# A selective scan's first steps reordered: single delta steps in a spare tile, sums ahead of layer 0's last pieces, late weights loaded one by one

## The chip, the core and the metric

The kernel runs on one core of a Trainium2 chip. A core has five engines that run side by side, each with its own queue of instructions taken in order: TensorE (PE, matmuls into PSUM), VectorE (DVE), ScalarE (ACT), GpSimd (POOL) and SyncE (SP, which here only issues DMA transfers). The metric is device time in microseconds (us) of one execution, from three executions before the change: 904.06, 905.18 and 905.91 us, median 905.18.

## The reference

Two transformer-like layers over four sequences (b) of 256 tokens with 512 features. Layer 0 adds to x a latent attention of 32 heads and a gated feed-forward part. Layer 1 adds a selective state-space block and a mixture of low-rank experts. Only the state-space block, and the end of layer 0 before it, matter here:

```
proj = hidden @ in_proj_w;  x, z = split(proj)          # 1024 channels each
xc = silu(conv4(x))                                     # causal, 4 taps a channel
dt_r, Bm, Cm = rmsnorm of the parts of xc @ x_proj      # 32, 16, 16
dt = softplus(dt_r @ dt_proj + dt_bias)                 # the "delta steps"
h[t] = exp(dt[t] * A) * h[t-1] + dt[t] * Bm[t] * xc[t]  # per channel and 16 states
y[t] = sum over states of h[t] * Cm[t]
out = ((y + D * xc) * silu(z)) @ out_proj
```

softplus(v) is made as relu(v) + log(1 + exp(-|v|)), with a correction for the rounding of 1 + exp(-|v|).

## The kernel before

**Layer 0's end.** The feed-forward down projection of the second half of the tokens (`down(1, i)`, blocks 4 to 7 of 128 tokens) is a generator of 64 pieces: for each block one piece with the attention part (L437), fourteen pieces of two 128x512 matmuls (L442), and one that adds the result to x (L447) or, for the last blocks, leaves it in PSUM for `add_last` (L454). `go(ff, n)` puts the next n pieces into TensorE's queue. They are used as filling between layer 1's first work, by hand: 9 before the convolution, then 1 between its parts, 8, 3, 9, then 12 in each of steps 0 and 1, and the rest in step 2.

**The scan.** The 1024 channels of a sequence are 8 chunks (c) of 128; a chunk takes 4 steps, each for 4 of the 16 states, so that a sequence has 32 steps and the kernel 128. A step u works on tiles whose 128 partitions are 32 channels x 4 states, with four such blocks of 256 tokens side by side, and its parts lie on four engines:

- ACT: `decays` makes exp(dt * A) (L867), two steps ahead of the scan;
- DVE: `scan_in` makes bx (L873), then `scan` makes h with one scan instruction (L888);
- POOL: hc = h * C (L892);
- TensorE: `states_sum` adds hc over the states into ysum (L904), one step later; the D part (L902) opens a chunk.

After a chunk's last step `close_chunk` (L908) multiplies ysum by silu(z) (sz, made by `gate_silu`, which loads ACT's silu table and then the exponential one again). The channels of a chunk must be spread over partitions in another layout: dt and du = dt * xc are sent to DRAM (`send`, L821) and read back in pieces (`spread`, four issues each, L827) as dts and dus. Chunk 0 of the first sequence goes through TensorE instead (pdts, pdus: L1080, L1087), and chunk 1 is sent alone (L1092).

**Delta steps.** `step_in` makes a matmul pdt for two chunks and |v| and relu(v) on ACT (L784, L785); `step_exp` makes the exponential, 1 + it, and the logarithm on ACT (L793 to L796), in the tiles u, lw and e; `step_out` makes three sums on POOL, and `step_x` du on POOL. For chunks 2 and 3 of the first sequence this is done with chunk pairs: the first two before step 0 (L1100, L1101), the sums on POOL in steps 0 to 2.

**Borrowed tiles.** Layer 0's tiles lie where layer 1's large pool (`act`) will be. Until layer 0's last matmul is done, the first four steps borrow other tiles (L847): their decays, h and hc lie in the weight tiles w_in, and in u, lw and e. `open_act` (L1103) then closes layer 0's pool, makes decay tiles 1 and 2, and loads the weights for the end of the layer: rl, bw, lb and ow, 0.27, 1, 0.25 and 2 MB, one behind the other on SP (L1112).

**What else the first sequence's steps hold.** The loads of the z weights (`load_z`, 0.5 MB into w_in) and the matmuls pz from them (L836); the second sequence's layer norm (`norm_stats`, `norm_scale` with sh on DVE, L668, and xnt on ACT, `norm_turn`, `norm_copy`), its input projection px (L696) and convolution (ACT L704 to L712, DVE L720, POOL L726).

**The order.** Nothing is scheduled automatically: each engine's queue is the order in which the program calls. `put(b, s, f)` hangs a call into step s of sequence b ahead of the step's scan, `put_late` behind it, and one loop over the steps walks these lists:

```
for u in range(total + 2):
    if u < 2: go(ff, 12)
    if 3 <= u < total - 2: decays(u + 2)
    ... put calls, scan_in, close_chunk, scan ...
    if u == 2: open_act()
    if u < 3: decays(u + 2)
    ... put_late calls ...
    if 1 <= u <= total: states_sum(u - 1)
```

Of the kernel before, what the change touches and what calls it, by code (L numbers as in the profile page):

```python
# [8 lines left out]
F32 = mybir.dt.float32  # L9
# [8 lines left out]
P = 128  # L18
# [23 lines left out]
def block_kernel(  # L42
# [389 lines left out]
    def down(th, i):  # L432

        tb = 4 * th + i
        po = psmm.tile([P, D], F32, tag="mm", name="po")
        for hf in range(2):
            mm(po, lhsT=o8ns[th][:, hf, i * P : (i + 1) * P], rhs=m_att[:, hf, :],  # L437
               start=(hf == 0), stop=False)
        yield
        for m in range(MC):  # L440
            for j in range(2):
                mm(po, lhsT=hids[th][j][:, m, i * P : (i + 1) * P], rhs=wd[:, m, :],  # L442
                   start=False, stop=(m == MC - 1 and j == 1))
            if m < MC - 1 or th:
                yield
        if tb < 6:
            nc.vector.tensor_tensor(x[:, tb, :], x[:, tb, :], po, ALU.add)  # L447
        else:
            live["last", tb] = po
        yield  # L450
# [5 lines left out]
    def go(gen, n=1000):  # L456
        for _ in range(n):
            if next(gen, 1) == 1:
                break
# [327 lines left out]
    def step_exp(b, h, q=slice(0, 4)):  # L787
# [7 lines left out]
        nc.scalar.activation(e, w, AF.Identity, bias=eps[:, 2:3])  # L795
        nc.scalar.activation(w, w, AF.Ln)  # L796

    def step_out(b, h, q, k):
        s = slice(2 * q, 2 * q + 2)
        e, dt = live["e"][:, s, :], dts[b, h][:, s, :]  # L800
        if k == 0:
            nc.gpsimd.tensor_tensor(e, live["u"][:, s, :], e, ALU.subtract)
        elif k == 1:
            nc.gpsimd.tensor_tensor(e, e, live["lw"][:, s, :], ALU.add)
        else:
            nc.gpsimd.tensor_tensor(dt, dt, e, ALU.add)
            send("dt", b, 2 * h + q, dt)
# [11 lines left out]
    def send(n, b, p, t):  # L819
        live[n, b, p] = scr.tile([2, P, S], F32, tag=n, name=f"{n}d")  # L820
        nc.sync.dma_start(live[n, b, p].rearrange("c p t -> p c t"), t)  # L821
# [17 lines left out]
    def gate_silu(b, *ps):  # L839
# [5 lines left out]


    lent = {  # L847
        "d": ("d", "w_in", "d", "w_in"), "h": ("w_in", "u", "w_in", "u"),
        "hc": ("w_in", "lw", "e", "lw"),
    }  # L850

    def lend(n, u):
# [218 lines left out]
    for j, eng in ((0, nc.vector), (1, nc.gpsimd)):  # L1071
# [1 line left out]
        eng.tensor_tensor(e[:, j, :], e[:, j, :], lw[:, j, :], ALU.add)  # L1073
        eng.tensor_tensor(dt[:, j, :], dt[:, j, :], e[:, j, :], ALU.add)
        eng.tensor_tensor(du[:, j, :], dt[:, j, :], xcs[0][:, j, :], ALU.mult)
    go(ff, 9)

    pdts = psx.tile([P, NG, S], F32, tag="bx", name="pdts")
    for k in range(NG):
# [17 lines left out]
    b_rows(0, 1)  # L1097
    c_rows(0, 1)
    decays(1)
    step_in(0, 0, 1)  # L1100
    step_exp(0, 0, slice(2, 4))  # L1101

    def open_act():  # L1103
        nonlocal act
        l0.close()
        act = ctx.enter_context(tc.tile_pool(name="act", bufs=1))
        decay_tile(act)
        decay_tile(act)
        for n, shape, d in (("rl", [P, HC, NE + P], rl_d), ("bw", [P, HC, D], base_d),
                            ("lb", [P, D], lb_d), ("ow", [P, DC, D], ow_d)):  # L1110
            late_w[n] = act.tile(shape, F32, name=n)
            nc.sync.dma_start(late_w[n], d)  # L1112


    at, late_at = {}, {}
# [1 line left out]
    def put(b, s, f, *a):  # L1117
        at.setdefault(b * PER + s, []).append((f, a))

    def put_late(b, s, f, *a):  # L1120

        late_at.setdefault(b * PER + s, []).append((f, a))

    for b in range(B):
        nxt = b + 1
        if b:
            put(b, 0, b_rows, b, 1)
            put(b, 0, spread, "du", b, 1)

            for c in range(DC):  # L1130
                put(b, c // 2, out_mm, b - 1, 1, c)
            put(b, 3, out_x, b - 1, 1)
            put(b, 4, dense, b - 1, 0, 0)
            put(b, 5, dense, b - 1, 0, 1)
            put(b, 5, expert_out, b - 1, 0)
            for c in range(DC):
                put(b, 6 + c, out_mm, b - 1, 0, c)
            put(b, 15, out_x, b - 1, 0)
        else:
            for k in range(3):  # L1140
                put(b, k, step_out, b, 0, 1, k)
            put(b, 2, step_x, b, 1)
            put(b, 1, load_z, b, 0)
            put(b, 4, load_z, b, 1)
            for p, u in ((0, 2), (1, 6)):
                for i in range(2):
                    put(b, u, pz_mm, b, p, i)
            put(b, 2, go, ff)
            put(b, 4, gate_silu, b, 0)
            put(b, 8, gate_silu, b, 1)  # L1150
            put_late(b, 2, add_last, 6)
            put_late(b, 3, add_last, 7)
        if b:
            put(b, 0, gate_silu, b, 0, 1)

        o = 0 if b else 3
        put(b, 1 if b else 5, step_in, b, 1, 0)
        put(b, 2 if b else 6, step_in, b, 1, 1)
        put(b, 3 if b else 7, step_exp, b, 1)
        for q in range(2):  # L1160
            for k in range(3):
                put(b, 5 + o + 3 * q + k, step_out, b, 1, q, k)
        for p in (2, 3):
            put(b, 3 * p + 2 + o, step_x, b, p)
        for c in range(2, DC):
            o = 0 if b or c < 4 else 1
            put(b, 4 * c - 6 + o, spread, "dt", b, c)
            put(b, 4 * c - 4 + o, spread, "du", b, c)
        put(b, 10, load_z, b, 2)
        put(b, 12, load_z, b, 3)  # L1170
        for p, at_i, at_g in ((2, (14, 15), 16), (3, (19, 21), 23)):
            for i in range(2):
                put(b, at_i[i], pz_mm, b, p, i)
            if p == 3 or nxt == B:
                put(b, at_g, gate_silu, b, p)
        if nxt < B:
            o = 0 if b else 1
            put(b, 0 if b else 2, norm_stats, nxt)
            put(b, 2 + o, norm_scale, nxt)
            put(b, 3 + o, norm_turn, nxt, 0)  # L1180
            put(b, 4 + o, norm_copy, nxt, 0)
            put(b, 4 + o, norm_turn, nxt, 1)
            put(b, 5 + o, norm_copy, nxt, 1)
            for p in range(NP):
                put(b, 2 * p if b else (5, 6, 7, 8)[p], load_x, nxt, p)
                for i in range(2):
                    put(b, 6 + o + 2 * p + i, px_mm, nxt, p, i)
                put(b, 8 + o + 2 * p, conv_in, nxt, p)
                put(b, 9 + o + 2 * p, conv_taps, nxt, p)
            put(b, 16 + o, conv_silu, nxt, (b, 2))  # L1190
            put(b, 17 + o, pp_mm, nxt, 0)
            put(b, 18, pp_mm, nxt, 1)
            put(b, 19, pp_square, nxt)
            put_late(b, 20, pp_norm, nxt)
            put(b, 21, step_in, nxt, 0, 0)
            put(b, 22, step_in, nxt, 0, 1)
            put(b, 22, c_rows, nxt, 0)
            put(b, 23, step_exp, nxt, 0)
            put(b, 23, c_rows, nxt, 1)
            for q in range(2):  # L1200
                for k in range(3):
                    put(b, 24 + 3 * q + k, step_out, nxt, 0, q, k)
            put(b, 27, step_x, nxt, 0)
            put(b, 27, spread, "dt", nxt, 0)
            put(b, 29, spread, "du", nxt, 0)
            put(b, 30, step_x, nxt, 1)
            put(b, 30, b_rows, nxt, 0)
            put(b, 31, spread, "dt", nxt, 1)
            put(b, 23, load_z, nxt, 0)
            put(b, 25, load_z, nxt, 1)  # L1210
            for k, u in enumerate((27, 28, 29, 31)):
                put(b, u, pz_mm, nxt, k // 2, k % 2)
            if b % 2 == 0:
                for i, u in enumerate((16, 17, 18, 20)):
                    put(b, u, router, b, i)
                put(b, 22, route_exp, b)
                put(b, 23, route, b)
            put(b, 24, expert_turn, b)
            put(b, 25, dense, b, 1, 0)
            put(b, 26, dense, b, 1, 1)  # L1220
            put(b, 27, expert_out, b, 1)
        else:

            put(b, 12, expert_turn, b)
            put(b, 17, dense, b, 0, 0)
            put(b, 18, dense, b, 0, 1)
            put(b, 18, expert_out, b, 0)
            put(b, 20, dense, b, 1, 0)
            put(b, 21, dense, b, 1, 1)
            put(b, 21, expert_out, b, 1)  # L1230
# [1 line left out]
    total = B * PER  # L1232
    late = []
    for u in range(total + 2):
        if u < 2:
            go(ff, 12)
        if 3 <= u < total - 2:
            decays(u + 2)
        for f, a in at.get(u, ()):
# [9 lines left out]
                late.append(c)  # L1249
        if u < total:  # L1250
            scan(u, 1 if u < total - 1 else 4)
            if u == 2:
                open_act()
            if u < 3:
                decays(u + 2)
        for f, a in late_at.get(u, ()):
            f(*a)
# [3 lines left out]
                out_mm(B - 1, i, c)  # L1261
        if 1 <= u <= total:
            states_sum(u - 1)
    for i in range(2):
        for c in late:
            out_mm(B - 1, i, c)
        out_x(B - 1, i)
# [101 lines left out]
```

## Time and profile before

| what | value |
|---|---|
| median of three runs | 905.18 us |
| the profiled execution's own time | 904.87 us |
| its span, from first to last instruction | 903.1 us |
| PE, DVE, ACT, POOL busy | 749.8, 687.3, 525.4, 489.1 us |
| TensorE clock granted, mean | 0.93 |
| scan of step 0, 1, 2, 3, 4 starts (DVE L888) | 362.85, 369.70, 378.22, 384.23, 388.37 us |
| scan of step 5, 8, 9, 10, 16 starts | 393.44, 404.46, 414.91, 426.24, 452.23 us |
| layer 0's last matmul ends | 384.8 us |
| one bx, scan, hc, decay (four ACT instructions) | 1.24, 2.29, 2.35, 1.7 us |

All times of single instructions are in us from the start of the span of one profiled execution. In a timeline a line gives the start, the duration, the engine, the source line, the operation, what it writes and reads, and in brackets how long the engine had been idle before it and what ended that. In the chain of waits, a line is one stretch of the work that ended last, in order of time: start, duration, engine and line.

### The profile page before, as it was taken

Reading aid. Unit: us, or ns where it says so; the run is one execution under the profiler, and the core shown is the slowest. Engines: PE = TensorE matmul, PEld = TensorE weight load, DVE = VectorE, ACT = ScalarE, POOL = GpSimd, SP = SyncE. Lnnn points to the kernel's source line nnn. Section 1 sums busy time; section 2 is a strip of 40 time slices with the busy share of each in tenths; the row PEclk is TensorE's granted clock in tenths of the full one; section 3 lists DMA queues with packets and bytes.
Section 4 is the critical chain, followed back from the end, with each engine's and each line's share of the span. In section 5 each row is a group of like instructions: output and inputs, shape, how many; then the busy total and the mean of one; then the engine's idle time right before and its main releaser. Section 6 shows DMA issues by size and latency. Waiting matters only on the chain.

```text
span 903.1 us, 10448 instructions
## 1 busy us (share of the span) xinstructions
PE 749.8 (83%) x3554; PEld 432.4 (48%) x3554; DVE 687.3 (76%) x675; ACT 525.4 (58%) x1005; POOL 489.1 (54%) x374
## 2 busy tenths in 40 slices
PE   5999979999989999956785798787897877875875
PEld 3665545666556576733452434443444443322421
DVE  5685553476563423694998999999999999999996
ACT  4234455313437346468778497778687785765661
POOL 4222222001223341554965969868789749797664
PEclk9899999999999999969796999987999888989997
DMA  6232332001122241493523443632645323436300
GB/s 210 60 92 72 81 105 70 12 1 36 48 69 70 59 109 31 116 275 110 142 58 93 127 142 103 165 94 62 171 120 170 85 79 84 117 94 169 87 26 23
DMA packets 67343, 86.67 MB, mean 96 GB/s; under 512 B 12077, under 2 KB 52025, under 8 KB 66906
## 3 DMA queue, kind: packets, MB, share of 16 engines
q1 hardware_dynamic: 57930, 67.12, 26.6%
q0 software_dynamic: 9072, 18.35, 7.4%
q8 instruction: 28, 0.46, 0.2%
q10 hardware_dynamic: 288, 0.52, 0.2%
q14 instruction: 25, 0.20, 0.1%
HBM read 66.58 MB, written 10.22 MB: 85 GB/s over the span
## 4 chain that ended last, share of the span: by engine, by line
PE 38%; DVE 33%; ACT 15%; issue 4%; POOL 4%; DMA 4%; SPq 1%; DVEq 0%; ACTq 0%; POOLq 0%
DVE h L888 20%; ACT decay L867 7%; DVE bx L873 6%; PE po L442 5%; PE pu L417 5%; PE pg L417 4%; PE sc L329 4%; PE av L371 3%; PE scT L361 3%; PE pz L836 2%; POOL hc L892 2%; PE pp L740 2%; DMA w_in<-in_inz 1%; ACT pe L363 1%; PE ysum L904 1%
## 5 line engine op out<-in xcount | busy, mean ns | idle before, releaser
L892 POOL TENSOR_TENSOR hc<-h,cr 128x1024 f32<-128x1024 f32 (+1 forms) x131 | 301.8, 2306 | 111.0 <-DVE h L888 96.3
L888 DVE TENSOR_TENSOR_SCAN h<-decay,bx 128x1024 f32<-128x1024 f32 (+1 forms) x129 | 287.9, 2234 | 15.1 <-PE ysum L904 3.5
L867 ACT ACTIVATE decay<-dts,aneg 128x255 f32<-128x255 f32 x504 | 213.9, 498 | 130.3 <-DVE h L888 115.6
L904 PE MATMUL ysum<-hc,stack 128*32 128x256 f32 x1024 | 89.8, 420 | 94.9 <-POOL hc L892 94.5
L873 DVE TENSOR_TENSOR bx<-brow,dus 128x1024 f32<-128x1024 f32 x128 | 157.6, 1231 | 3.7
L429 POOL TENSOR_TENSOR hlo<-g,hhi 128x512 fp32r<-128x512 f32 x28 | 36.1, 1289 | 149.3 <-ACT hhi L428 149.3
L331 DVE TENSOR_REDUCE mpl<-sc 128x4 f32<-128x1024 f32 x64 | 77.2, 1222 | 23.9 <-PE sc L329 23.8
L904 PEld LDWEIGHTS ysum<-hc,stack 128*32 128x32 f32 x1024 | 21.6, 111 | 154.0 <-POOL hc L892 137.2
L400 POOL DMA_DIRECT2D wgu<-in_wgu x56 | 31.0, 553 | 92.4 <-PE pg L417 82.3
L363 ACT ACTIVATE pe<-scT 128x1024 f32<-128x1024 f32 x64 | 62.8, 1023 | 29.8 <-PE scT L361 29.5
L996 PE MATMUL po<-ow,xc 128*128 128x512 f32 x128 | 72.3, 674 | 2.7 <-DVE xc L908 2.7
L836 PE MATMUL pz<-xn1T,w_in 128*128 128x256 f32 x256 | 69.7, 421 | 4.4 <-DMA w_in<-in_inz 4.4
L696 PE MATMUL px<-xn1T,w_in 128*128 128x256 f32 x256 | 63.4, 394 | 2.2 <-ACT xn1T L688 1.6
L836 PEld LDWEIGHTS pz<-xn1T,w_in 128*128 128x128 f32 x256 | 50.5, 207 | 24.2 <-issue 11.1
L696 PEld LDWEIGHTS px<-xn1T,w_in 128*128 128x128 f32 x256 | 49.9, 198 | 21.6 <-issue 11.0
L425 DVE SCALAR_TENSOR_TENSOR g<-g,pg 128x512 f32<-128x512 f32 x28 | 19.2, 685 | 52.0 <-ACT g L424 52.0
L428 ACT CAST hhi<-g 128x512 fp32r<-128x512 f32 x28 | 17.4, 620 | 62.1 <-DVE g L427 61.8
L417 PE MATMUL pg<-xhi,wgu 128*128 128x512 f32 x112 | 46.8, 418 | 5.4 <-issue 2.9
L417 PE MATMUL pu<-xhi,wgu 128*128 128x512 f32 x112 | 47.8, 426 | 3.3 <-issue 1.5
L442 PE MATMUL po<-wd,hhi 128*128 128x512 f32 x112 | 48.8, 435 | 0.0
L329 PE MATMUL sc<-km,qg 128*128 128x512 f32 x128 | 43.9, 424 | 3.3 <-ACT pe L363 2.8
L417 PE MATMUL pg<-xlo,wgu 128*128 128x512 f32 x112 | 44.9, 401 | 0.0
(214 smaller groups left out, 1251.9 us busy)
## 6 DMA issues: line engine op xcount, KB each, us to landing
dts<-dtd SPq DMA_DIRECT2D x124, 128.0 KB, 2.9
dus<-dud SPq DMA_DIRECT2D x124, 128.0 KB, 3.0
wgu<-in_wgu POOLq DMA_DIRECT2D x56, 256.0 KB, 2.8
w_in<-in_inz SPq DMA_DIRECT2D x16, 512.0 KB, 4.8
w_in<-in_inx SPq DMA_DIRECT2D x15, 512.0 KB, 4.6
dtd<-dt SPq DMA_DIRECT2D x15, 256.0 KB, 2.2
dud<-du SPq DMA_DIRECT2D x15, 256.0 KB, 2.2
wd<-in_wd POOLq DMA_DIRECT2D x7, 512.0 KB, 3.6
```

Source lines behind the costliest of these rows:

```text
L329: mm(sc[:, hp, :], lhsT=qs[b][:, gq, hf, qb * P : (qb + 1) * P], rhs=kms[b][:, 2 * hp : 2 * hp + 2, :], start=True, stop=True)
L331: nc.vector.tensor_reduce(mpl2[b % 2][:, qb, :, 16 + 2 * gq + hf].rearrange("p (a i) -> p a i", a=2), sc.rearrange("p a (i k) -> p a i k", ...
L417: mm(ps, lhsT=wgus[i][:, hc, :], rhs=xs[j][:, hc, :], start=(hc == 0 and j == 0), stop=(hc == HC - 1 and j == 1))
L442: mm(po, lhsT=hids[th][j][:, m, i * P : (i + 1) * P], rhs=wd[:, m, :], start=False, stop=(m == MC - 1 and j == 1))
L696: mm(px[:, i, :], lhsT=w[:, i, hc, :], rhs=xns[b][:, hc, :], start=(hc == 0), stop=(hc == HC - 1))
L836: mm(pz[:, i, :], lhsT=w[:, i, hc, :], rhs=xns[b][:, hc, :], start=(hc == 0), stop=(hc == HC - 1))
L867: nc.scalar.activation(da[:, k, 1:], live["dts", b, c][:, k, 1:], AF.Exp, scale=aneg[:, c, k, g : g + 1])
L873: nc.vector.tensor_tensor(bx, brow[g // 2][:, g % 2, :].unsqueeze(1).to_broadcast([P, NG, S]), live["dus", b, c], ALU.mult)
L888: nc.vector.tensor_tensor_scan(h[:, n].rearrange("p n t -> p (n t)"), da[:, n].rearrange("p n t -> p (n t)"), bx[:, n].rearrange("p n t -> ...
L892: nc.gpsimd.tensor_tensor(hc[:, n], h[:, n], crows[b][:, g, :].unsqueeze(1).to_broadcast([P, NG // parts, S]), ALU.mult,)
L904: mm(ysum[k * NB : (k + 1) * NB, :], lhsT=stack, rhs=hc[:, k, :], start=False, stop=(g == NU - 1))
L996: mm(live["po", b, i], lhsT=xcs[b][:, c, i * P : (i + 1) * P], rhs=late_w["ow"][:, c, :], start=False, stop=(c == DC - 1))
```

## The change

- Ahead of pdts there are 5 pieces of layer 0 and not 9. In step 0, 9 pieces are put in, in step 1, 12, in step 2 the rest, each behind the step's scan and behind `states_sum` of the step before, not ahead of it. Block 5's sum joins those of `add_last`.
- The delta steps of chunks 2 and 3 are made one chunk at a time by `one_step` and `one_out`, in a tile `one` that has the convolution's tag "tap" (one buffer) in place of u, lw and e.
- In the first four steps h of step 2 lies in e and hc of step 2 in w_in (the other way round before).
- `open_act` makes the tiles of the late weights but doesn't load them; `load_late` loads rl, bw, lb and ow in steps 9, 11, 13 and 15. `open_act` and the decays of step 4 come at the end of step 2, behind the last pieces.
- `load_z` 0 comes behind step 2's scan, followed by the sends; the spread of chunk 2's dt in step 3; pz 0 in step 3; the norm statistics of the second sequence behind step 3's scan, its `norm_scale` and the first `norm_turn` one step or so later, the `norm_copy` calls behind the scan of step 5.

```diff
-        if tb < 6:
+        if tb < 5:
             nc.vector.tensor_tensor(x[:, tb, :], x[:, tb, :], po, ALU.add)
         else:
             live["last", tb] = po
...
+    def one_step(c):
+        pd = psmm.tile([P, 2, S], F32, tag="mm", name="pdt")[:, 0, :]
+        mm(pd, lhsT=dtw[:, c * P : (c + 1) * P], rhs=nrms[0][0:RK, :], start=True, stop=True)
+        t = live["one"] = w1.tile([P, KC - 1, S], F32, tag="tap", name="one")
+        u, w, e = (t[:, k, :] for k in range(3))
+        db = vec[:, c, V_DB : V_DB + 1]
+        nc.scalar.activation(u, pd, AF.Abs, bias=db)
+        nc.scalar.activation(dts[0, 0][:, c, :], pd, AF.Relu, bias=db)
+        nc.scalar.activation(u, u, AF.Exp, scale=-1.0)
+        nc.scalar.activation(w, u, AF.Identity, bias=1.0)
+        nc.scalar.activation(e, w, AF.Identity, bias=eps[:, 2:3])
+        nc.scalar.activation(w, w, AF.Ln)
+
+    def one_out(c):
+        u, w, e = (live["one"][:, k, :] for k in range(3))
+        dt = dts[0, 0][:, c, :]
+        nc.gpsimd.tensor_tensor(e, u, e, ALU.subtract)
+        nc.gpsimd.tensor_tensor(e, e, w, ALU.add)
+        nc.gpsimd.tensor_tensor(dt, dt, e, ALU.add)
...
     lent = {
-        "d": ("d", "w_in", "d", "w_in"), "h": ("w_in", "u", "w_in", "u"),
-        "hc": ("w_in", "lw", "e", "lw"),
+        "d": ("d", "w_in", "d", "w_in"), "h": ("w_in", "u", "e", "u"),
+        "hc": ("w_in", "lw", "w_in", "lw"),
     }
...
-    go(ff, 9)
+    go(ff, 5)
...
-    step_in(0, 0, 1)
-    step_exp(0, 0, slice(2, 4))
+    one_step(2)
...
-            late_w[n] = act.tile(shape, F32, name=n)
-            nc.sync.dma_start(late_w[n], d)
+            late_w[n] = act.tile(shape, F32, name=n), d
+
+    def load_late(n):
+        t, d = late_w[n]
+        nc.sync.dma_start(t, d)
+        late_w[n] = t
...
-            for k in range(3):
-                put(b, k, step_out, b, 0, 1, k)
-            put(b, 2, step_x, b, 1)
-            put(b, 1, load_z, b, 0)
+            put(b, 1, one_out, 2)
+            put(b, 1, one_step, 3)
+            put(b, 2, one_out, 3)
+            put_late(b, 2, load_z, b, 0)
+            put_late(b, 2, lambda: send("dt", 0, 1, dts[0, 0][:, 2:4, :]))
+            put_late(b, 2, step_x, b, 1)
             put(b, 4, load_z, b, 1)
-            for p, u in ((0, 2), (1, 6)):
+            for k, n in enumerate(("rl", "bw", "lb", "ow")):
+                put(b, 9 + 2 * k, load_late, n)
+            for p, u in ((0, 3), (1, 6)):
                 for i in range(2):
                     put(b, u, pz_mm, b, p, i)
-            put(b, 2, go, ff)
             put(b, 4, gate_silu, b, 0)
             put(b, 8, gate_silu, b, 1)
-            put_late(b, 2, add_last, 6)
-            put_late(b, 3, add_last, 7)
+            put_late(b, 1, add_last, 5)
+            put_late(b, 3, add_last, 6)
+            put_late(b, 4, add_last, 7)
...
-            put(b, 4 * c - 6 + o, spread, "dt", b, c)
+            put(b, 3 if c == 2 and not b else 4 * c - 6 + o, spread, "dt", b, c)
...
-            put(b, 0 if b else 2, norm_stats, nxt)
-            put(b, 2 + o, norm_scale, nxt)
-            put(b, 3 + o, norm_turn, nxt, 0)
-            put(b, 4 + o, norm_copy, nxt, 0)
-            put(b, 4 + o, norm_turn, nxt, 1)
-            put(b, 5 + o, norm_copy, nxt, 1)
+            if b:
+                put(b, 0, norm_stats, nxt)
+            else:
+                put_late(b, 3, norm_stats, nxt)
+            put(b, 2 if b else 4, norm_scale, nxt)
+            put(b, 3 if b else 5, norm_turn, nxt, 0)
+            (put if b else put_late)(b, 4 if b else 5, norm_copy, nxt, 0)
+            put(b, 4 if b else 5, norm_turn, nxt, 1)
+            (put if b else put_late)(b, 5, norm_copy, nxt, 1)
...
     for u in range(total + 2):
-        if u < 2:
-            go(ff, 12)
...
             scan(u, 1 if u < total - 1 else 4)
-            if u == 2:
-                open_act()
-            if u < 3:
+            if u < 2:
                 decays(u + 2)
         for f, a in late_at.get(u, ()):
             f(*a)
...
         if 1 <= u <= total:
             states_sum(u - 1)
+        if u < 3:
+            go(ff, (9, 12, 100)[u])
+        if u == 2:
+            open_act()
+            decays(4)
```

## The prediction

> **What bounds the kernel now.** I read the page, then the chain of waits and each engine's timeline from 350 to 500 us, the only stretch the edits touch. Of the page:
>
> ```profile
> span 903.1 us, 10448 instructions
> PE 749.8 (83%) x3554; PEld 432.4 (48%) x3554; DVE 687.3 (76%) x675; ACT 525.4 (58%) x1005; POOL 489.1 (54%) x374
> ```
>
> From about 424 us DVE is hardly idle (449.75 of the 479 us to the end busy; bx 1.24 and scan 2.29, 3.66 us a step), so a scan that starts earlier there ends the kernel earlier. Before that it isn't the bound: step 0's scan starts at 362.85 and step 10's at 426.24, 63.4 us where ten steps need 36.6. DVE's timeline shows the holes:
>
> ```profile
> 369.70 2.29 DVE L888 TENSOR_TENSOR_SCAN h<-d,bx 128x1024 f32<-128x1024 f32 x1 [3.30 <-POOL e L802]
> ...
> 378.22 2.29 DVE L888 TENSOR_TENSOR_SCAN h<-decay,bx 128x1024 f32<-128x1024 f32 x1 [3.51 <-PE ysum L904]
> ...
> 414.57 0.42 DVE L908 TENSOR_TENSOR xc<-ysum,sz 128x256 f32<-128x256 f32 x1 [6.55 <-PE ysum L904]
> ...
> 423.46 1.01 DVE L720 SCALAR_TENSOR_TENSOR px<-pad,vec,px 128x256 f32<-128x256 f32 x2 [6.28 <-ACT xc L707]
> ```
>
> The chain of waits names what is under the last two: a weight load issued behind the late weights (L1112), then TensorE, then ACT.
>
> ```profile
> 387.17 13.18 DMA w_in<-in_inz
> 400.34 0.14 issue
> 400.48 5.78 PE pz L836 x16
> 406.25 1.07 PE pdt L779 x4
> 407.32 0.02 issue
> 407.35 0.03 ACT u L784
> ```
>
> ACT's timeline shows its two long waits there:
>
> ```profile
> 384.86 3.30 ACT L867 ACTIVATE decay<-dts,aneg 128x255 f32<-128x255 f32 x8 [10.71 <-PE po L442]
> ...
> 407.35 0.47 ACT L784 ACTIVATE u<-pdt,vec 128x256 f32<-128x256 f32 x1 [7.75 <-PE pdt L779]
> ```
>
> And the issues of this stretch, with us to landing (the load above took 13.2):
>
> ```profile
> w_in<-in_inz SPq DMA_DIRECT2D x6, 512.0 KB, 4.8
> ...
> ow<-in_ow SPq DMA_DIRECT2D x1, 2048.0 KB, 11.4
> ```
>
> **What the Trainium skill says.** "TensorE: Matmul & The Clock Gate", What's actually happening: after an idle window of about 3.4 us TensorE runs at half clock, and at full again after such a time of sustained work. The trace agrees: the windows from 393 to 401 show a clock of 0.50, from 405 on 1.00, and L836 took 5.78 us at 400.48 but 3.72 at 377.92. The same page, Architectural detail, calls ACT's and DVE's queues strict FIFO: here DVE stood 6.55 us at L908 with its scan behind it. "DMA: Bandwidth & Descriptors", Queues, rings and completion order: each DMA engine takes a queue's descriptors in ring order; the 13.18 us beside a usual 4.8 agree.
>
> **The change, part by part** (times on the clock of the profile).
>
> *Five pieces instead of nine before pdts.* The 16 L442 matmuls at 353.37 end at 357.15; ten end at 355.75 (0.23 each), after DVE's dt (355.06). pdts, its copy, bx and scan 0 come 1.4 us earlier: scan 0 at 361.45. Block 5's sum (0.67) leaves an idle place on DVE for one behind scan 1. The sends of chunk 1 don't move (POOL's chain, 358.2).
>
> *Single steps in a spare tile.* ACT: twice 2.49 us (351.12 to 353.61 for chunk 0's six) for 4.06 (364.81 to 368.87); POOL: six of 0.81 for three of 1.28, plus 1.0. But POOL's hc 0 now stands directly behind scan 0 (363.8 to 366.2; before, 369.63), and the u tile is free, so the POOL wait of the first DVE line goes: scan 1 at 361.45 + 3.65 = 365.1. A new wait: the spare tile has one buffer, so ACT's second step waits for POOL's third add on the first (366.2 + 3 x 0.8 = 368.6); queued behind it on ACT is decay 3 (368.6 + 2.5 + 1.65 = 372.75), for which DVE asks at 372.8.
>
> *Sums in front of the pieces, h of step 2 in the e tile.* hc 0 is summed at 368.5 (before 377.35), and scan 2 no longer needs its buffer: with the moved sum of 0.67, scan 2 at 369.25 (378.22), scan 3 at 372.9 (384.23), 11 us ahead.
>
> *Where that gain goes.* Decays 1 and 2 lie in the pool that opens when layer 0's last matmul is done (the 10.71 above). TensorE is busy without a gap from 353.37 to 384.83, 31.5 us; pz 0 (3.65) now follows the pieces and ysum 1 (0.57) precedes the last of them, so 28.4, and it ends near 381.9: 2.9 earlier only. What its new order makes it wait for is early: hc 0 (366.2) for ysum 0, hc 1 (368.6 + 2.4) for ysum 1 at 375, block 5's sum (368.0) for the place of block 7's po at 373. ACT's decays 4 and 5 (3.3) and then rsn (0.52) end at 385.75. DVE's sh (L668) now stands ahead of bx 4 and waits for rsn; Four statistics moved behind scan 3 (1.7) fall into that hole. sh itself took 0.13 twice and 1.98 once under a POOL hc; POOL is idle then, so 0.13. bx 4, scan 4 at 387.3, against 388.37: 1.1 left of 11. Block 7's sum, sz and close 0 put scan 5 at 391.6 (393.44).
>
> *z 1 without the late weights.* The four L1112 issues (1.7 us) leave SP's queue there, and dts of chunk 2 goes out behind dud with z 1 behind it; z 0 is issued after step 2, not in step 1. On SP: z 0 after ysum 0 (368.6), dtd (373.5), dud behind POOL's hc 2 and du (377.2), chunk 2's dts, z 1 at 379.5, dus; z 1 lands near 384 (4.8), dts and dus of chunk 2 by 385, and decay 8 asks at 396. x 0 (behind pz 0, 385.7, landing 390.5) and x 1 (behind decay 7 and ysum 2, 395.8, landing 400.6) are early for the px matmuls of 403 to 409. So pz 1 waits for something else: the PSUM place that ACT frees. ACT from 385.75: decay 6 (1.65), table, sz, table (3.2), two xnt (1.5), decay 7 (1.65), four steps of pdt (1.45): 395.2. pz 1 starts 5.3 us earlier than 400.48. TensorE idles some 3.6 us from 387.8, as it did before, so I take its 5.78 and pdt's 1.07 again; bounds 3.65 (full clock) and 7.3 with 2.1 (half throughout). ACT's second four steps: 402.1 (407.35).
>
> *From there ACT sets the pace, as before*: 407.35 to the taps at 423.46 is 16.1 us, less one xn1T copy (0.46), now ahead of decay 8: taps at 417.75, 5.7 us earlier. close 1 waits for ysum 7, which TensorE reaches behind pdt, two ysum and two half px (402.1 + 5.6 = 407.7), so it is done by 408.1, scan 9 by 410.5, and both hide in front of the taps.
>
> *rl, bw, lb, ow in steps 9 to 15.* Four issues of 0.4 us on SP, where it waits anyway. On the old clock ow goes out at 446.8 right before dts of chunk 5, for which ACT asks at 461.4: 14 us. Both together: at the rate of the old burst (3600 KB from 385.2 to 398.0) 2560 KB take 9 us; above, 11.4 + 2.9 = 14.3; below, an estimate by the page's 2.0 us plus bytes over 436 GB/s (Anatomy of one DMA, given for the other DMA path): 8. So nothing; that cover gone, each us late is a us on ACT and the scans. dus of chunk 5 waits for ow's landing too and has till 465.7. rl (step 16) and bw (step 25) are early.
>
> Sum: nothing before 353, -5.7 at step 10, kept over the DVE-bound rest. The profiled execution took 904.87 (span 903.1 and 1.8 around it): 899.2. The median is 0.3 above it: 905.18 - 5.7 = **899.5 us**.
>
> **Rivals.**
> *Warm*: TensorE keeps its clock, pz 1 takes 3.65: 2.1 more, 897.4. For: there is work at 391 to 394; against: the old idle of 3.1 us cooled it.
> *Cold*: half clock through pz 1 and pdt, second four steps at 404.6: 3.1 gained, 902.1. For: before, the clock came back only after some 4 us of work; against: it did come back within pz.
> *No gain*: the cause of the 6.28 lies in ACT's own queue and something that I put at nothing (z 1 behind dud, rsn later, x 0 behind pz 0) takes the 5.3 again: within 1.8 us of 905.2. For: ACT has 15.6 us of work there whatever DMA does; against: each of these has 5 us or more to spare, but for rsn.
> *Slower*: ow's 2 MB hold dts and dus of chunk 5 in the ring, DVE stands before step 20. It cancels the gain at 14.2 + 5.7 = 20 us from issue to landing and is slower by 1.8 from 22; at 24, 909. For: the same weights delayed z 1 by 8 us; against: then four of them, here one with a smaller load behind.
> *The change doesn't do what it says*: z 1 still late; excluded by SP's order, in which no late weight stands ahead of it.
>
> **How the numbers follow.** 0.2% (1.8 us) is about what a measurement can tell. Forecast (gain 4.5 to 6.8) 0.50, warm 0.20, cold 0.14, no gain 0.09, slower 0.07. So faster 0.84, same 0.09, slower 0.07. The range takes in warm with 0.9 of spread and cold with the same: 896.5 to 903.0; the forecast's own is 898.4 to 900.7.
>
> **What would show it.** Scan 1 without a POOL wait, near 365; scan 3 near 373; then a hole of about 8 us on DVE up to sh at 385.8 (wait on ACT rsn). ACT's decay 4 at 382 behind PE po. z 1 landing in about 5 us; pz 1 released by ACT, near 395; ACT's wait for the second pdt down from 7.75 to 2 to 5 us; taps near 417.8; the same distances from there. I am wrong if scan 4 is later than 388.4, if pz 1 starts after 398, if DVE waits for dts or dus in steps 18 to 20, or if the gain of step 10 isn't there at the end.

## The result, and the profile after

The kernel after takes 898.48 us (median of four runs, 897.88 to 899.43), the kernel before beside it 904.62 (903.00 to 905.91). The ratio is 0.9934, with a 95% interval of 0.9915 to 0.9953: faster by 6.1 us, between 0.5 and 0.9%. The forecast was 899.5, its own range 898.4 to 900.7.

The page of the kernel after, its first lines; the busy time of the engines has hardly moved (DVE 687.3 to 685.5), the span is 6.2 us shorter:

```profile
span 896.9 us, 10459 instructions
PE 752.1 (84%) x3554; PEld 433.4 (48%) x3554; DVE 685.5 (76%) x675; ACT 526.3 (59%) x1009; POOL 490.3 (55%) x377
```

DVE's timeline after (start, duration, instruction, and in brackets the idle time before it and what ended that):

```profile
365.38 2.29 DVE L909 TENSOR_TENSOR_SCAN h<-d,bx 128x1024 f32<-128x1024 f32 x1 [0.19 <-DMA dts<-dtd]
...
373.18 2.29 DVE L909 TENSOR_TENSOR_SCAN h<-d,bx 128x1024 f32<-128x1024 f32 x1
...
386.50 0.16 DVE L668 SCALAR_TENSOR_TENSOR sh<-mv,rsn 128x2 f32<-128x2 f32 x1 [8.84 <-ACT rsn L652]
...
388.01 2.29 DVE L909 TENSOR_TENSOR_SCAN h<-decay,bx 128x1024 f32<-128x1024 f32 x1
...
416.34 1.01 DVE L720 SCALAR_TENSOR_TENSOR px<-pad,vec,px 128x256 f32<-128x256 f32 x2 [6.99 <-ACT xc L707]
```

POOL's wait at scan 1 is gone, and so are the 3.51 us at scan 2 and the 6.55 us at close 1. Scan 3 starts 11.05 us earlier than before (384.23), scan 4 only 0.36 us earlier (388.37): the lead ends in the hole ahead of sh. What is left of the gain appears at the taps, 7.1 us earlier than before (423.46). The chain of waits names what lies between:

```profile
376.11 6.61 PE po L442 x28
382.72 0.02 issue
382.75 3.30 ACT decay L888 x8
...
395.89 3.72 PE pz L857 x16
399.61 1.07 PE pdt L779 x4
400.68 0.02 issue
400.70 0.03 ACT u L784
```

No transfer stands in this stretch any more; before, 13.18 us of z 1's load did. ACT's timeline has the same two waits as before, the second a third as long (7.75 before):

```profile
382.75 3.30 ACT L888 ACTIVATE decay<-dts,aneg 128x255 f32<-128x255 f32 x8 [9.81 <-PE po L442]
...
400.70 0.47 ACT L784 ACTIVATE u<-pdt,vec 128x256 f32<-128x256 f32 x1 [2.31 <-PE pdt L779]
```

From step 10 (scan 7.12 earlier) the distances stay as they were up to 734 us, where the gain is 6.94. Two places then give back 0.34 and 0.47 us: the second router pass, where DVE waits 1.40 us for ACT's ex where it waited 1.06, and a pz at 765.60 that TensorE did at half clock, in 3.78 us, where before it took 1.99 (at 771.75). The end is 6.1 earlier.

### The profile page after: what moved, and what is told of

Same layout as the page of the kernel before. It is cut to its first block, busy times and chain, and to the rows that moved or that the text cites. A ratio compares the mean times of both kernels' runs of the same rounds, so it can differ in the third digit from the quotient of the medians.

```text
span 896.9 us, 10459 instructions
## 1 busy us (share of the span) xinstructions
PE 752.1 (84%) x3554; PEld 433.4 (48%) x3554; DVE 685.5 (76%) x675; ACT 526.3 (59%) x1009; POOL 490.3 (55%) x377
## 4 chain that ended last, share of the span: by engine, by line
PE 39%; DVE 36%; ACT 14%; issue 5%; POOL 4%; DMA 1%; DVEq 0%; ACTq 0%; POOLq 0%
DVE h L909 21%; DVE bx L894 7%; ACT decay L888 6%; PE po L442 5%; PE pu L417 5%; PE pg L417 4%; PE sc L329 4%; PE av L371 3%; PE scT L361 3%; POOL hc L913 2%; PE pz L857 2%; PE pp L740 2%; PE px L696 2%; PE ysum L925 1%; ACT pe L363 1%
## 5 line engine op out<-in xcount | busy, mean ns | idle before, releaser
L696 PE MATMUL px<-xn1T,w_in 128*128 128x256 f32 x256 | 65.8, 406 | 0.8 <-DMA w_in<-in_inx 0.7
L428 ACT CAST hhi<-g 128x512 fp32r<-128x512 f32 x28 | 17.3, 620 | 61.9 <-DVE g L427 61.6
L442 PE MATMUL po<-wd,hhi 128*128 128x512 f32 x112 | 48.5, 433 | 0.0
```

The lines of the kernel that those rows point to most:

```text
L696: mm(px[:, i, :], lhsT=w[:, i, hc, :], rhs=xns[b][:, hc, :], start=(hc == 0), stop=(hc == HC - 1))
```

## The experiments

Each was timed against the kernel before, whose medians lay between 904.36 and 904.91; times of single instructions are from one profiled execution of each. The start of step 0's scan, up to which all kernels with the early edits have the same program, lay anywhere from 360.10 to 362.46 in their profiles, so two profiles are compared by distances within each where a microsecond matters. A profile shows one execution out of 4 to 22, and it ends up to 3.3 us off the median of its kernel; the last section shows a reason.

### Late loads without the rest, and the rest without the late loads

**late_together**: the kernel after, its four loads together again.

```diff
-            late_w[n] = act.tile(shape, F32, name=n), d
+            late_w[n] = act.tile(shape, F32, name=n)
+            nc.sync.dma_start(late_w[n], d)
...
-            for k, n in enumerate(("rl", "bw", "lb", "ow")):
-                put(b, 9 + 2 * k, load_late, n)
```

> The kernel after, with rl, bw, lb and ow loaded together again where the act pool is opened. Theory (the later loads carry most of the gain): SP stands at rl until layer 0's last matmul (382.7), the burst takes 12.8 us as before, z 1 lands 15.1 us after its start as before, near 398, pz 1 is cold again (5.78 for 3.72), so the second four steps of ACT come 4 to 6 us later than the 400.70 of the kernel after: 902.5 to 904.5 us in all. Rival (the single steps and the sums in front carry the gain): no more than 1 us slower than the kernel after, 898.5 to 899.5.

Measured: 904.36 us, ratio 0.9998 (0.9984 to 1.0011). The whole gain is gone, at the upper end of what the theory expected. Scan 3 still starts at 372.82, so the 11 us of lead that it has there over the kernel before are worth nothing by themselves. The chain of waits of late_together:

```profile
386.55 13.06 DMA w_in<-in_inz
399.61 0.14 issue
399.74 6.66 PE pz L857 x16
```

z 1 lands at 399.6, 1.6 later than expected and about where it did before (400.3), and pz 1 then takes 6.66 us, 0.9 more than before. ACT's second four steps begin at 407.49 (before: 407.35).

**late_alone**: the kernel before, with the four loads moved to steps 9 to 15 and nothing else.

```diff
-            late_w[n] = act.tile(shape, F32, name=n)
-            nc.sync.dma_start(late_w[n], d)
+            late_w[n] = act.tile(shape, F32, name=n), d
+
+    def load_late(n):
+        t, d = late_w[n]
+        nc.sync.dma_start(t, d)
+        late_w[n] = t
...
+            for k, n in enumerate(("rl", "bw", "lb", "ow")):
+                put(b, 9 + 2 * k, load_late, n)
```

> The kernel before, with nothing changed but that rl, bw, lb and ow are loaded one by one in steps 9, 11, 13 and 15. Theory: z 1 lands near 391 instead of 400.3, pz 1 then waits for ACT's fourth step of pdt, which ends at 397.5 in the kernel before; second four steps at 402.3 (pz 1 at full clock) or 404.4 (cold), against 407.35: 3 to 5 us faster than before, 899.6 to 901.7, the rest up to the kernel after being the 2.1 us by which layer 0's last matmul ends earlier there. Rival: without the early steps ACT isn't ready and nothing is gained, 904.6.

Measured: 902.14 us, ratio 0.9974 (0.9964 to 0.9984): 2.5 us faster, a little under the 3 to 5 expected, and 3.7 short of the kernel after. The chain of waits of late_alone:

```profile
396.08 0.36 ACT u L784
396.44 0.38 ACT dt L785
396.82 0.04 issue
396.86 5.66 PE pz L836 x16
```

As expected, pz 1 waits for ACT's fourth step and no longer for its weights, and TensorE is cold. The second four steps come at 403.62, against 400.70 in the kernel after. Of these 2.92 us, 1.94 are pz 1's duration (5.66 against 3.72) and 0.97 its start; with the 0.46 of the xn1T copy that stands behind the steps here and ahead of them after, the taps (419.75 against 416.34) account for the missing 3.7 us but for 0.3.

So neither part makes the gain alone: 0 and 2.5, but 6.1 together. With the burst in place, the early edits make ACT ready for a pz 1 whose weights are late; with the weights in time, pz 1 waits for ACT, which the early edits bring forward. By the figures above, though, more than half of what they add to late_alone is the clock at pz 1 and not ACT's start; which of the early edits that hangs on, and how much of it is chance, wasn't separated.

### Which of the delayed transfers counted

**z1_ahead**: late_together with z 1's load ahead of the burst.

```diff
             put_late(b, 2, step_x, b, 1)
-            put(b, 4, load_z, b, 1)
+            put_late(b, 2, load_z, b, 1)
```

> late_together, but with z 1's load issued behind step 2's transfers, directly ahead of rl, bw, lb and ow, instead of behind them. Theory (of all that the burst delays, only z 1 counted): z 1 lands near 382, pz 1 starts at 395.9 when ACT frees its place, at full clock; dts of chunk 2 costs ACT 0.6 ahead of decay 8, dus and x 0 up to 1 us: 898.5 to 899.5 us, as the kernel after, against 904.4 of late_together. Rival (the burst costs by dts, dus and x 0 as well): at least 2 us slower than the kernel after, above 900.5.

Measured: 897.66 us, ratio 0.9930 (0.9906 to 0.9955), which isn't to be told from the kernel after. The weights may be loaded in one burst, as long as z 1 isn't behind it. TensorE's timeline of z1_ahead shows what else the burst delayed:

```profile
396.71 3.72 PE L857 MATMUL pz<-xn1T,w_in 128*128 128x256 f32 x16
...
403.64 3.61 PE L696 MATMUL px<-xn1T,w_in 128*128 128x256 f32 x8 [1.58 <-DMA w_in<-in_inx]
```

x 0 was 1.58 us late for px (up to 1 was expected), and px ran at half clock behind it; ACT's conv, which takes px at 415.39, stands later still and hid both. dts of chunk 2 was 0.73 us late for ACT (0.6 expected), which ACT had to wait for pdt anyway.

**late_in_15**: all four loads of the kernel after in step 15.

```diff
-                put(b, 9 + 2 * k, load_late, n)
+                put(b, 15, load_late, n)
```

> The kernel after, with rl, bw, lb and ow all issued in step 15 (one behind the other at 439.7) instead of in 9, 11, 13 and 15, directly ahead of dts of chunk 5. Theory (there are 14 us of cover, and the old burst's rate puts 3600 KB and dts at 14.6): dts of chunk 5 lands near 454.6, for which ACT asks at 454.3, so 0 to 1.5 us are lost: 898.5 to 900. Rival (the forecast's slower case: the ring holds dts and dus for 20 us and more): DVE stands ahead of step 20 by 6 us or more, above 904.

Measured: 899.18 us, ratio 0.9929 (0.9906 to 0.9952); no difference from the kernel after can be seen. ACT's timeline of late_in_15, the decay of step 20:

```profile
454.17 1.70 ACT L888 ACTIVATE decay<-dts,aneg 128x255 f32<-128x255 f32 x4 [0.57 <-DMA dts<-dtd]
```

dts of chunk 5 is 0.57 us late on ACT, and the scan of step 20 doesn't move (it follows the one before at the usual 3.69). The cover was as large as the prediction worked it out: 3600 KB and dts use it up, ow alone doesn't. What a still larger load would do wasn't tried.

### What sets the pace from 382 to the taps

**norm_early**: batch 1's norm in ACT's idle time ahead of layer 0's last matmul.

```diff
-                put_late(b, 3, norm_stats, nxt)
-            put(b, 2 if b else 4, norm_scale, nxt)
+                put_late(b, 2, norm_stats, nxt)
+            (put if b else put_late)(b, 2, norm_scale, nxt)
```

> The kernel after, with batch 1's statistics, rsn, sh and xnt made behind scan 2, so that ACT does rsn (0.5) and xnt (1.4) in its idle 9.81 us before layer 0's last matmul instead of behind it. Theory (from 382.75 to the taps ACT's own work sets the pace; the lead of scan 3 is worth nothing): scan 3 2.4 later, near 375.6; DVE no longer waits for rsn, scan 4 near 384.6 instead of 388.01; pz 1 at 394.0 instead of 395.89; end 1.9 earlier, 896.6 us, or 898.7 if TensorE is cold at pz 1. Rival (the early scans set the end): the 3.4 us of scan 4 are kept, 895.1; or scan 3's delay is, 900.9.

Measured: 897.38 us, ratio 0.9927 (0.9900 to 0.9954), not to be told from the kernel after. Scan 4 starts at 384.05, 4 us earlier, and its idle time is ended by its decay, no longer by rsn. The gain is lost at pz 1. TensorE's timeline of norm_early:

```profile
390.19 0.64 PE L925 MATMUL ysum<-hc,stack 128*32 128x256 f32 x8
393.56 6.78 PE L857 MATMUL pz<-xn1T,w_in 128*128 128x256 f32 x16 [2.73 <-ACT dt L785]
```

pz 1 starts 2.3 us earlier than in the kernel after and takes 3.06 longer, so the taps come at 417.07 instead of 416.34. This is the expectation's cold case, with 1.0 more than it took for it. That the profiled execution still ends 1.83 us before that of the kernel after isn't gained here: it comes later, 1.68 us of it from the clock (last section).

**norm_early_busy**: the same, TensorE's idle time filled with transposes that write the same values again.

```diff
-        for hc in range(HC):
+        for hc in list(range(HC)) * (6 if b == 1 and i == 1 else 1):
             nc.tensor.transpose(pt[:, hc, :], live["xnt", b][i][:, hc * P : (hc + 1) * P], ident)
```

> norm_early with the four transposes of xnt's second half made six times over on TensorE (the same values into the same place, 20 extra), which fill its idle 2.73 us ahead of pz 1. Theory (pz 1 took 6.78 us there and 3.72 in the kernel after because TensorE had cooled in those idle us): pz 1 starts near 393.7 as before and takes 3.7, second four steps near 398.4 instead of 401.44, and all from there 3.0 earlier: 894.3 us against 897.4. Rival (pz 1's time isn't a matter of the idle time ahead of it): 6.8 again, 897.4 us or more by what the extra transposes delay.

Measured: 895.16 us, ratio 0.9895 (0.9871 to 0.9920); 2.2 us faster than norm_early by the medians. The intervals overlap, and three of the six executions took 892.7 to 893.0, the other three 897.3 to 898.5 (the profiled one 898.48), so the ends alone don't settle it. TensorE's timeline of norm_early_busy does:

```profile
389.50 2.84 PE L680 MATMUL pt<-cst,xnt 128*128 128x128 f32 x24 [0.80 <-ACT sz L863]
...
393.97 3.72 PE L857 MATMUL pz<-xn1T,w_in 128*128 128x256 f32 x16 [0.62 <-ACT dt L785]
```

With 2.84 us of transposes, 20 of 24 needed by nobody, pz 1 is 3.06 us shorter, and no window around it shows a lower clock: 6.78 was a matter of the clock alone. The taps come at 414.42, 2.65 earlier than in norm_early.

**pdt_first**: the kernel after, with pdt's second half ahead of pz 1 on TensorE.

```diff
-            for p, u in ((0, 3), (1, 6)):
-                for i in range(2):
-                    put(b, u, pz_mm, b, p, i)
+            for i in range(2):
+                put(b, 3, pz_mm, b, 0, i)
...
         put(b, 2 if b else 6, step_in, b, 1, 1)
+        if not b:
+            for i in range(2):
+                put(b, 6, pz_mm, b, 1, i)
```

> The kernel after, with the 16 matmuls of pz 1 behind the second four matmuls of pdt on TensorE instead of ahead of them. Theory: pdt then runs at 395.9 to 397.0 and ACT goes on with its steps right behind decay 8, at 398.3 instead of 400.70 (its wait of 2.31 gone); taps near 413.9 instead of 416.34; end 2.4 earlier, 896.1 us. Rival (something else than ACT holds the taps, TensorE's px halves or POOL): under 0.5 us gained.

Measured: 896.06 us, ratio 0.9910 (0.9889 to 0.9932), 2.4 us faster than the kernel after by the medians. ACT's second four steps start at 398.55 with no wait ahead of them, and the taps at 414.20, both 2.15 earlier than in the kernel after although step 0 was 0.27 later. So the order of two groups of matmuls on TensorE was worth the whole 2.31 us that ACT waited.

**both**: norm_early and pdt_first together.

> norm_early and pdt_first together: batch 1's norm in ACT's idle time, pdt's second half ahead of pz 1. Theory (ACT's own work paces 382.75 to the taps): pdt is cold (2.1 us from 393.6), ACT's second four steps at 396.1 right behind decay 8 (398.55 in pdt_first), taps near 411.8 instead of 414.2; pz 1 takes 6.8 cold and ends at 402.5, 4 us before its silu; 893.7 us. Rival (a cold pz 1 delays the px matmuls behind it, and these hold ACT's conv): no better than pdt_first, 896.1 us.

Measured: 893.64 us, ratio 0.9875 (0.9855 to 0.9895). ACT's steps begin at 396.03, the taps at 411.68 (expected 396.1 and 411.8). The cold pz 1 (6.47 at 395.29) holds ysum back, so that close 1 waits, but the taps still wait for ACT. DVE's timeline of both:

```profile
407.38 0.42 DVE L929 TENSOR_TENSOR xc<-ysum,sz 128x256 f32<-128x256 f32 x1 [3.29 <-PE ysum L925]
...
411.68 1.01 DVE L720 SCALAR_TENSOR_TENSOR px<-pad,vec,px 128x256 f32<-128x256 f32 x2 [1.69 <-ACT xc L707]
```

**both_busy**: both, with the extra transposes.

> The kernel of the run both, with the same 20 extra transposes as in norm_early_busy. Theory: the clock that they keep up makes pdt 1 us and pz 1 3 us shorter, but ACT's steps stand behind decay 8 until 396.1 anyhow and the silu of pz 1 is later still: the same time as both within 0.4 us, 893.7 us. Rival (TensorE's time at pz 1 is on the path there too): 1 to 3 us faster than both.

Measured: 892.90 us, ratio 0.9874 (0.9853 to 0.9894), the same as both. TensorE kept its clock: pz 1 took 3.72. DVE's taps in both_busy:

```profile
411.16 1.01 DVE L720 SCALAR_TENSOR_TENSOR px<-pad,vec,px 128x256 f32<-128x256 f32 x2 [5.01 <-ACT xc L707]
```

They stand 50.46 us behind scan 0 (at 360.70), in both 50.45 (361.23). A pz 1 shorter by 2.75 us, worth 2.65 at the taps in norm_early, is worth nothing where ACT doesn't wait for it: it makes DVE's idle time longer, 5.01 for 1.69.

### The order on DVE at the taps

**taps_later**: the kernel after, with one pair's taps a step later.

```diff
-                put(b, 9 + o + 2 * p, conv_taps, nxt, p)
+                put(b, 9 + o + 2 * p + (not b and p == 0), conv_taps, nxt, p)
```

> The kernel after, with batch 1's first taps (two of 1.01 us and one of 0.48 on DVE) put in step 11 instead of step 10, so that they stand behind scan 10 on DVE; ACT's conv stays in its place. Theory (DVE stands idle 6.99 us at the taps for ACT while decay 10 is made at 409.76): scan 10 near 410.7 instead of 419.12, the taps still at 416.3, scan 11 one step of 3.66 earlier, and the end too: 894.9 us. Rival (ACT's pace, not the order on DVE, holds the steps behind the taps as well): under 1 us, 897.5 to 898.5.

Measured: 894.95 us, ratio 0.9889 (0.9866 to 0.9912), 3.5 faster than the kernel after. DVE's timeline of taps_later:

```profile
410.34 2.29 DVE L909 TENSOR_TENSOR_SCAN h<-decay,bx 128x1024 f32<-128x1024 f32 x1 [0.58 <-POOL hc L913]
415.93 1.01 DVE L720 SCALAR_TENSOR_TENSOR px<-pad,vec,px 128x256 f32<-128x256 f32 x2 [3.30 <-ACT xc L707]
...
418.70 2.29 DVE L909 TENSOR_TENSOR_SCAN h<-decay,bx 128x1024 f32<-128x1024 f32 x1
```

Scan 10 now fills the hole ahead of the taps, and the scan behind them is that of step 11, which started at 422.77 in the kernel after. ACT paced the taps, but not the scans: these were late because they stood behind the taps in DVE's queue. The edit itself is worth less than the step of 3.66 expected: the second pair's taps now wait 0.96 us for ACT, which leaves some 2.7 (estimate). From step 12 on the scans stand 3.01 us ahead of those of the kernel after; 1.19 of this was there at scan 0, and pz 1 took 0.75 longer here, so the profile gives 2.6. The rest of the 3.5 isn't explained by the taps.

**both_taps_later**: the same edit in both.

> The kernel of the run both, with the taps of batch 1's first pair in step 11 instead of step 10. There DVE waits 3.29 us for ysum in close 1, so scan 9 ends at 410.0 and taps begin at 411.7: of a step of 3.66, 1.7 us lie in the idle time. Theory: 1.7 us earlier than both, 892.0 us. Rival (as in taps_later): no change, 893.6 us.

Measured: 891.39 us, ratio 0.9846 (0.9822 to 0.9871), 2.25 faster than both by the medians and 13 faster than the kernel before: the best of the kernels here. The taps start at 412.40 without a wait.

## Why the prediction was right, and where a term was off

**Steps 0 to 3.** Right within 0.3 us: scan 0 at 361.64 (predicted 361.45), scan 1 at 365.38 (365.1), scan 2 at 369.49 (369.25), scan 3 at 373.18 (372.9). That is closer than two profiles agree on scan 0 (360.10 to 362.46), so in part chance; the distances from scan to scan, free of that, are right within 0.1 us (3.74, 4.11 and 3.69, for 3.65, 4.15 and 3.65). The new wait was there too: ACT's second single step was let go by POOL's third add, at 368.75 (368.6).

**Where the lead goes.** Right in place, and late_together shows that it is worth nothing by itself. TensorE ended layer 0 at 382.7, not 381.9. The chain gives 72 matmuls of L442 in both kernels: they took 17.3 us instead of 16.7 (in five stretches now, before in four; why they took longer stays open), and ysum's D part and the single pdts 0.4 more than I had moved. All that follows on ACT was 0.7 late: rsn at 386.46 (385.75), scan 4 at 388.01 (387.3), pz 1 at 395.89 (395.2).

**z 1 without the late weights.** Right: issued at 379.46 (379.5), and pz 1 was let go by ACT. z 1 took 6.4 us beside dts and dus, not 4.8, so it landed at 385.9, with 10 us to spare. late_together and z1_ahead show that this one load carried the harm of the burst.

**The term that was mis-sized: pz 1's clock.** The sentence was "TensorE idles some 3.6 us from 387.8, as it did before, so I take its 5.78 and pdt's 1.07 again". The idle time was about as forecast, 3.93 us up to 392.15, and the transposes did run cold (1.97 us for 8). But pz 1 took 3.72: the clock was back at 395.1, before it began. That is the rival *Warm*, 2.06 us better. "As it did before" didn't hold: before, TensorE stood idle twice more ahead of pz 1 (1.91 us, then 4.38 for its weights), here only 0.30. With the 0.7 us by which pz 1 was late, the second four steps came at 400.70 instead of 402.1 and the taps at 416.34 instead of 417.75. late_alone (5.66) and norm_early (6.78) had the cold case; norm_early_busy shows that the duration hangs on the clock.

**ACT's pace.** Right: 15.64 us from the second four steps to the taps (15.65 taken). norm_early_busy, pdt_first and both moved ACT's work or wait there, and the taps followed. What the prediction took for granted is that scan 10 had to come behind the taps; taps_later, 3.5 us faster by the medians, shows what lay in that.

**rl, bw, lb, ow.** Right: ow went out at 439.73 (446.8 less the gain of 7.1) and landed in 8.4 us, DVE waited for nothing in steps 18 to 20, and late_in_15 measures the cover.

**The sum.** The 7.1 us at step 10 were more than the 5.7 forecast, and 6.1 are left at the end, since 1.0 was given back as told above. That the end came within 1.0 us of the forecast is thus partly two deviations that cancelled, a warm pz 1 and losses to the router's wait and the clock late in the kernel. The warm pz 1 is itself in part luck: with the same order of work ahead of it, it took 4.47 in taps_later and 4.45 in late_in_15.

## What to carry to other kernels

A lead that an engine gets ahead of a fixed point (here the last matmul of layer 0) is worth only what the work behind that point can use: ask first what ends the wait there, then what fills the idle time in front of it. A large load that nobody needs yet does harm through the one small load behind it in the same queue; put the small one ahead, or the large one later with its cover in us worked out. Where an engine waits for another in strict order, look whether something that is ready stands behind the waiting instruction: two such swaps (pdt ahead of pz 1, scan 10 ahead of the taps) gave 2.4 and 3.5 us here by the medians, and cost nothing.

## What the runs showed of the hardware

TensorE's clock falls and comes back in steps of 3.4 us. In the kernel after it changes at 391.64, 395.05, 412.12 and 415.53 (each placed by the mean clock of its window of 0.2 us): 3.41, 17.07 and 3.41 apart, which is one step, five and one. Windows of the kernel after and then of taps_later, which has the same order of work on TensorE up to there (window, length, busy us and instructions of PE, PEld, DVE, ACT and POOL, granted clock, DMA share, GB/s):

```profile
391.00:392.00 1.00, 0.00 (x0) 0.00 (x0) 1.00 (x2) 0.99 (x2) 1.00 (x1) 0.82 0.00 0
392.00:393.00 1.00, 0.85 (x4) 0.85 (x5) 1.00 (x3) 1.00 (x3) 0.73 (x1) 0.50 0.00 0
...
394.00:395.00 1.00, 1.00 (x7) 0.35 (x10) 0.97 (x2) 1.00 (x3) 0.38 (x1) 0.50 0.00 0
395.00:396.00 1.00, 0.70 (x9) 0.22 (x10) 0.90 (x2) 1.00 (x4) 1.00 (x1) 0.97 0.48 148
```

```profile
389.00:390.00 1.00, 0.00 (x0) 0.00 (x0) 1.00 (x3) 1.00 (x1) 0.82 (x1) 0.73 0.00 0
390.00:391.00 1.00, 0.05 (x1) 0.05 (x1) 1.00 (x2) 0.99 (x3) 1.00 (x1) 0.50 0.00 0
...
395.00:396.00 1.00, 1.00 (x3) 0.82 (x4) 1.00 (x1) 1.00 (x4) 0.78 (x1) 0.50 0.82 253
396.00:397.00 1.00, 1.00 (x5) 0.84 (x5) 1.00 (x1) 1.00 (x3) 0.00 (x0) 0.86 0.74 187
```

In the kernel after, half clock lasted from 391.6 to 395.1, 3.4 us; in taps_later from 389.5 to 396.3, 6.8 us. Seen in windows of 0.2 us, the half-clock stretches around pz 1 lasted about 3.4 us or twice or four times as long: 13.7 in the kernel before and in late_alone, 6.8 in norm_early, both and late_in_15, 3.4 in pdt_first and both_taps_later; norm_early_busy had none. The Trainium skill says it ("TensorE: Matmul & The Clock Gate", What's actually happening): the clock is decided by a free-running window of 3413 ns, which doesn't start anew with the kernel. So what an idle time costs depends on where it falls in the window. After 3.93 us of it pz 1 took 3.72 in the kernel after and in z1_ahead, and 4.47 in taps_later; directly behind 2.73 us, 6.78 in norm_early, and with pdt in between 6.47 in both and 5.03 in both_taps_later. To take such a duration over from another kernel, as I did, is a guess; both ends belong in the range. The same page (Why this matters for your kernels) advises to keep idle gaps under some 3 us. Here a gap of 2.73 us was enough to lose the clock in norm_early: it fell at 392.97, and of the 3.4 us up to there TensorE had worked only 1.3 (to 390.83).

The clock decides a later place too. The second sequence's 16 matmuls pp near 452 us, from TensorE's timelines of norm_early, of the kernel after and of norm_early_busy:

```profile
453.10 3.67 PE L740 MATMUL pp<-xc,xpw 128*64 128x256 f32 x16 [0.87 <-ACT xc L729]
...
452.43 5.35 PE L740 MATMUL pp<-xc,xpw 128*64 128x256 f32 x16 [0.90 <-ACT xc L729]
...
450.45 6.57 PE L740 MATMUL pp<-xc,xpw 128*64 128x256 f32 x16 [0.88 <-ACT xc L729]
```

The granted clock there was 1.00 in norm_early, 0.50 from 454 to 456 in the kernel after and from 450 to 456 in norm_early_busy. From step 20 to step 24 norm_early's scans gain 1.68 us on those of the kernel after and norm_early_busy's lose 1.22, which are the differences of pp; in the ten other profiles the two agree within 0.02 us as well. So the end of a single execution holds up to 2.9 us that hang on TensorE's clock at pp. How pp ran in the executions without a profile isn't recorded, so a difference of 1 or 2 us between the medians of 4 to 6 executions is weak evidence by itself.

A tiny DVE operation was drawn out beside a large POOL operation: in norm_early sh (128x2) took 1.79 us from 373.48, and POOL's hc ran from 372.90 to 375.25; scan 3 was later by about 1.6 us for that. In the kernel before it was the same (1.98 us, to 382.98; hc to 382.96). In the kernel after, without POOL beside it, sh took 0.16. Whether hc held it, or what of it, wasn't tried.
